# Layer 1 in a written order, with its last sums bank by bank; layer 3's rows one bank behind; shorter layernorm runs

## The chip, the cores and the metric

One core of one Trainium2 chip runs the whole program. The core has TensorE (PE, matrix products into PSUM), VectorE (DVE, elementwise), ScalarE (ACT, activation functions and copies), GpSimd (POOL), and the SP queue, which issues most DMAs. An engine works through its own queue in order, and semaphores tie the queues together. The metric is the time of one execution on the device in microseconds; the kernel before takes 1995.79 us (median of 3 runs, 1994.71 to 1996.02).

## The reference, cut to what matters

Four graph layers on N = 2708 nodes with D = 128 features share one matrix `adj` (2708 x 2708, about 2.3% filled). After each comes a layernorm. The change is in layers 1 and 3.

```python
def _L1_gnn_ref(node_features, adj_matrix, recency_prior, ...):   # recency_prior is adj again
    messages = node_features @ W_msg + b_msg
    logits = (messages @ W_q) @ (messages @ W_k).T / scale + gate_bias
    gates_masked = sigmoid(logits) * adj_matrix * recency_prior
    aggregated = gates_masked @ messages
    updated = relu(concatenate([node_features, aggregated], axis=1) @ W_upd + b_upd)
    ...                                             # layernorm, gamma, beta
# layer 3: n = adj @ x; s = n @ W + b; x1 = s * sigmoid(s); the same again on x1;
# then x + the second result, layernorm, and this is the output
```

The kernel adds a residual, `x + layernorm(...)`, and normalises it again. Layer 0 sums a gelu over pairs of neighbours. Layer 2 works on all pairs in hyperbolic geometry, with a small "bias point" made of `L2_gnn_b` and two attention vectors. All arithmetic of layers 1 to 3 that matters here is float32.

## The kernel before, in words

Rows are cut into NT = 22 tiles of 128 (the last has 20), and the 2708 columns into six banks: five of 512 and one of 148, each a PSUM bank. A float32 product of 128x512 shows up in the profile as two PE records.

**Two ways of ordering.** Inside `tc.manual_schedule()` each engine gets its instructions as the Python text issues them. Elsewhere a planner orders them by its own priorities, so that later work may be placed among earlier work. Layer 0's loop, layer 2's pairs and ends, and layer 3 have a written order. Layer 1 is left to the planner.

**Layernorm.** `normalize` (lines 199 to 218) turns the even and odd statistics of `bn_stats` into a scale r and an offset per row: a chain of 13 short DVE instructions with one square root on ACT in the middle (`Values.sqrt` takes one Newton step after it). Then each tile of the run is scaled and shifted by one instruction: every third tile on ACT (line 216), the others on DVE (line 218). `Resnorm.all` does two runs of 11 tiles: `add` (normalise h, times gamma, plus xb, statistics of the sum) for both, then `end` (normalise x) for both. Layer 0's end calls the same parts by hand.

**Layer 1, start (lines 979 to 1003).** Per group of four tiles: transposes of x, a copy by ACT (xT), the product with W_msg (mT, bias added by ACT), the product with the joined W_q W_k (qT, copied by DVE) and the rows of messages `mrow` (line 1002, one product of 128 columns per tile).

**Layer 1, loop (lines 1011 to 1030).** For every tile j: load the rows of adjT; six products `lg` (line 1024), each turned into a sigmoid by ACT (line 1025); two DVE multiplications by `at` over all 2708 columns (lines 1027 and 1028); six products into one PSUM tile `acc` of six banks (line 1030). `lg` has two PSUM buffers, `w` has two SBUF buffers, `at` three. `Weights2` (lines 290 to 327) prepares layer 2's bias point: DMAs on SP and POOL, some twenty small DVE instructions, two ACT functions and two products; the text calls it at tiles 5, 11 and 16, and the planner places it.

**Layer 1, end (lines 1031 to 1046).** DVE copies the six banks to aggT; 44 products (xT with the upper and aggT with the lower half of W_upd, line 266) give the rows of h; DVE adds the bias, ACT takes relu, DVE the statistics; then `Resnorm.all`.

**Layer 3 (lines 1473 to 1594).** Twice: nT = x^T adjT summed over 22 tiles in six PSUM banks (line 1543). Ten tiles of adjT are held in SBUF, the others are streamed. The last tiles (3 in the first pass, 6 in the second) are taken bank by bank. `Swish.step(k)` follows bank k: ACT copies bank k (line 1502), PE multiplies bank k-1 by W (line 266), DVE adds the bias (line 268) and ACT takes the sigmoid (line 1512); the rows of bank k-2 are finished: in the first pass one multiplication, in the second pass (`finish`, lines 1564 to 1576) multiplication, residual, statistics and, whenever at least 8 tiles are complete, `normalize` and the output DMA.

At the very end the count of cases that layer 0's fast way could not handle is read by every engine (line 1600), and a branch skips the slow way.

Of the kernel before, what the change touches and what calls it, by code (L numbers as in the profile page):

```python
# [20 lines left out]
P = 128  # L21
# [18 lines left out]
def gnn_stack(ctx: ExitStack, tc: tile.TileContext, t, out: bass.AP):  # L40
# [158 lines left out]
    def normalize(dst, src, st, a, b, V, sq=None):  # L199

        even, odd = st[:, a:b, 1], st[:, a:b, 4]
        d = V.tt(even, odd, ALU.subtract)
        q = V.new(d)
        nc.vector.scalar_tensor_tensor(q, d, 0.25, d, op0=ALU.mult, op1=ALU.mult)  # L204
        m = V.tt(st[:, a:b, 2], st[:, a:b, 5], ALU.add)
        nc.vector.scalar_tensor_tensor(q, m, 1.0 / D, q, op0=ALU.mult, op1=ALU.add)  # L206
        r = V.recip(V.sqrt(V.ts(q, LN_EPS, ALU.add)))
        mu = V.ts(V.tt(even, odd, ALU.add), 0.5, ALU.mult)
        if sq is not None:
            nc.vector.scalar_tensor_tensor(sq[:, a:b], q, float(D), V.mul(r, r), op0=ALU.mult, op1=ALU.mult)  # L210
        off = V.new(d)
        nc.vector.scalar_tensor_tensor(off, mu, -1.0, r, op0=ALU.mult, op1=ALU.mult)  # L212
        for i in range(a, b):
            c = slice(i - a, i - a + 1)
            if i % 3 == 2:
                nc.scalar.activation(dst[:, i, :], src[:, i, :], AF.Identity, bias=off[:, c], scale=r[:, c])
            else:
                nc.vector.tensor_scalar(dst[:, i, :], src[:, i, :], r[:, c], off[:, c], op0=ALU.mult, op1=ALU.add)  # L218
# [71 lines left out]
    class Weights2:  # L290
        def __init__(self, pool):
            self.pool = pool

        def load(self):
            nc.sync.dma_start(out=w2[:, :D], in_=t["L2_WT"])
            self.vecs = self.pool.tile([P, 3, D], F32, name="y2_vecs")
            self.cols = self.pool.tile([P, 3], F32, name="y2_cols")
            for k, name in enumerate(("L2_gnn_b", "L2_gnn_att_wl", "L2_gnn_att_wr")):
                nc.gpsimd.dma_start(out=self.vecs[:, k, :], in_=t[name].partition_broadcast(P))
                nc.sync.dma_start(out=self.cols[:, k:k + 1], in_=t[name].rearrange("(p o) -> p o", o=1))  # L300
            self.w_rows = self.pool.tile([P, D], F32, name="y2_w_rows")
            self.prods = self.pool.tile([P, 3, D], F32, name="y2_prods")

        def products_with(self, dst, v):
            nc.vector.tensor_tensor(self.prods, self.vecs, v[:, None, :].to_broadcast([P, 3, D]), op=ALU.mult)
            nc.vector.tensor_reduce(dst, self.prods, AX.X, ALU.add)

        def turn(self, ps):
            nc.tensor.transpose(ps[:, :D], w2[:, :D], ident)
            nc.vector.tensor_copy(self.w_rows, ps[:, :D])  # L310

        def bias_point(self):
            V = Values(self.pool, "y2_")
            vecs, cols = self.vecs, self.cols
            sums3 = self.pool.tile([P, 3], F32, name="y2_sums")
            self.products_with(sums3, vecs[:, 0, :])
            bn = V.norm(sums3[:, 0:1])
            bth = V.act(bn, AF.Tanh)
            bk = V.mul(V.mul(bth, V.recip(bn)), V.shrink(bth))
            nc.vector.tensor_scalar(y, vecs[:, 0, :], bk, None, op0=ALU.mult)  # L320
            nc.vector.tensor_copy(vecs[:, 0, :], y)
            nc.vector.tensor_tensor(cols[:, 0:1], cols[:, 0:1], bk, op=ALU.mult)
            self.products_with(yw, y)

        def columns(self, ps):
            nc.tensor.matmul(ps[:, :3], self.w_rows, self.cols, start=True, stop=True)
            nc.vector.tensor_copy(w2[:, D:], ps[:, :3])
# [631 lines left out]
    def layers_1_to_3(top):  # L959

        with ExitStack() as l1:
# [6 lines left out]
            mrow = wp.tile([P, NT, D], F32, name="mrow")  # L968
# [7 lines left out]
            with ExitStack() as pre:  # L976
                psum = pre.enter_context(tc.tile_pool(name="ps_pre1", bufs=2, space=PSUM))

# [10 lines left out]
                for a, b, r in groups():  # L989
# [12 lines left out]
                    sums(mrow[:r, a:b, :], a, b, r, [(xT, w_msg)], psum, msg_br)  # L1002
                nc.gpsimd.tensor_tensor(xb, x, over_tiles(beta), op=ALU.add)

            with ExitStack() as att:
                gp = att.enter_context(tc.tile_pool(name="gates", bufs=2))
                pacc = att.enter_context(tc.tile_pool(name="ps_agg1", bufs=1, space=PSUM))
                plog = att.enter_context(tc.tile_pool(name="ps_log", bufs=2, space=PSUM))
                acc = pacc.tile([P, N], F32, name="acc")
                weights2 = Weights2(wp)  # L1010
                for j, r in enumerate(rows):
                    at = stream.tile([P, N], F32, name="at")
                    nc.sync.dma_start(out=at[:r, :], in_=adjT[j * P:j * P + r, :])
                    if j == NT // 4:
                        weights2.load()
                    elif j == NT // 2:
                        weights2.turn(plog.tile([P, BANK], F32, name="lg"))
                        weights2.bias_point()
                    elif j == NT * 3 // 4:
                        weights2.columns(plog.tile([P, BANK], F32, name="lg"))  # L1020
# [452 lines left out]
        with ExitStack() as l3:  # L1473
# [20 lines left out]
            class Swish:  # L1494
# [24 lines left out]
                def step(self, k):  # L1519

                    if k < len(banks):
                        self.out_of(k)
# [111 lines left out]
```

## Time and profile before

| what | us |
|---|---|
| median of 3 runs | 1995.79 |
| the profiled execution's own time | 1993.64 |
| its span, first to last instruction | 1991.8 |
| layer 0 with its layernorm, until x is complete | 0 to 930.4 |
| layer 1's start, until the last of the first tile's `lg` | 931.9 to 970.0 |
| layer 1's loop, first `lg` to last `acc` | 948.7 to 1196.4 |
| layer 1's end, from there to the first transpose for layer 2 | 1196.4 to 1235.3 |
| layer 2, until layer 3's first product | 1235.3 to 1747.9 |
| layer 3, until the issue of the last output DMA | 1747.9 to 1984.0 |

PE is busy for 84% of the span, DVE for 77%, ACT for 55%. The page's slices show each engine's busy share over time; the timeline shows single instructions with their start, duration and, in brackets, the idle time of the engine before them and what ended it.

### The profile page before, as it was taken

The page shows a single profiled execution, that of the slowest core. Times are in us where ns is not written, and L with a number is a line of the kernel's source. Part 1 is how long each engine was busy: PE and PEld are TensorE (multiplying, and loading weights), DVE is VectorE, ACT ScalarE, POOL GpSimd, SP SyncE. Part 2 cuts the span into 40 slices and gives each one's busy share as a digit, 9 for nine tenths or more (in the row PEclk, how much of TensorE's full clock was granted, in tenths as well). Part 3 has the DMA queues.
Part 4 walks back from the last instruction along what each step waited for, and adds up shares of the span by engine and source line. Part 5 has one row for each costly group of instructions (what it writes and reads, how often), then busy time and mean ns, then how long its engine had stood idle before and what let it go on. Part 6 is the DMA issues. An engine that isn't in the chain of part 4 may idle for free. (4 is left out here: it accounts for less than half of the span.)

```text
span 1991.8 us, 36394 instructions
## 1 busy us (share of the span) xinstructions
PE 1663.9 (84%) x14037; PEld 949.8 (48%) x14037; DVE 1526.7 (77%) x3500; ACT 1103.2 (55%) x1519; POOL 679.0 (34%) x429
## 2 busy tenths in 40 slices
PE   5899999999999999871999994689898983089995
PEld 4666666666666666550444334322232321044542
DVE  7899999999999999876564658699999997810105
ACT  3666676666666666542433323599998983300103
POOL 5677677677577677461000000021000350000000
PEclk9899999999999999995999996779998986589998
DMA  8666666666666676432243310022222217034330
GB/s 224 150 130 135 138 139 128 136 141 127 136 148 122 136 147 111 82 66 88 114 141 139 127 45 1 1 87 88 75 81 95 81 42 293 0 144 167 112 116 30
DMA packets 218359, 222.25 MB, mean 112 GB/s; under 512 B 28373, under 2 KB 204475, under 8 KB 211715
## 3 DMA queue, kind: packets, MB, share of 16 engines
q1 hardware_dynamic: 167038, 195.95, 32.4%
q0 software_dynamic: 51136, 23.88, 10.3%
q8 instruction: 112, 1.84, 0.4%
q14 instruction: 73, 0.59, 0.1%
HBM read 211.94 MB, written 7.83 MB: 110 GB/s over the span
## 5 line engine op out<-in xcount | busy, mean ns | idle before, releaser
L722 POOL DMA_INDIRECT far<-d_tab,ix x352 | 561.8, 1596 | 259.2 <-DVE W L823 112.8
L836 ACT ACTIVATE g<-sl 128x768 f32<-128x768 f32 x484 | 393.4, 813 | 257.9 <-PE sl L763 238.1
L758 PE MATMUL sl<-dA,S 124*128 124x153 f16 x4840 | 408.8, 232 | 10.3 <-DVE W L823 7.8
L758 PEld LDWEIGHTS <-S 124*128 124x128 f16 x4840 | 331.1, 98 | 80.2 <-issue 68.4
L774 PE MATMUL acc<-g,W 128*32 128x128 f32 x4840 | 206.0, 278 | 0.5 <-DVE W L823 0.5
L1227 POOL TENSOR_TENSOR at<-at,off 128x128 f32<-128x128 f32 (+1 forms) x22 | 70.3, 3213 | 336.0 <-DVE m L1256 171.4
L1543 PE MATMUL acc<-held,x 128*128 128x512 f32 (+1 forms) x240 | 99.5, 563 | 84.1 <-DVE x L218 84.1
L774 PEld LDWEIGHTS acc<-g,W 128*32 128x32 f32 x4840 | 140.9, 109 | 58.6 <-issue 54.6
L763 PE MATMUL sl<-s,same 50*128 50x384 f16 x968 | 162.0, 308 | 0.0
L268 DVE TENSOR_TENSOR g<-ps,row_L_gnn_b 128x512 f32<-128x512 f32 (+2 forms) x14 | 7.9, 573 | 197.0 <-PE ps L266 196.9
L1025 ACT ACTIVATE w<-lg,row_L_gnn_gate_bias 128x512 f32<-128x512 f32 (+1 forms) x132 | 80.8, 635 | 137.7 <-PE lg L1024 74.3
L1283 PE MATMUL accV<-m,X 128*128 128x512 f32 (+4 forms) x264 | 128.4, 628 | 33.6 <-DVE m L1273 29.2
L823 DVE TENSOR_TENSOR W<-sl,own 128x150 f32<-128x150 f32 x484 | 143.3, 300 | 14.3 <-ACT g L836 13.6
L1235 PE MATMUL ps<-XT 128*128 128x512 f32 (+4 forms) x264 | 143.2, 626 | 3.1 <-ACT m L1240 2.8
L648 DVE TENSOR_SCALAR S<-rk 124x1000 f16<-124x1000 bf16 (+1 forms) x330 | 134.0, 431 | 0.0
L718 DVE FIND_INDEX8 ix<-v,o 128x8 uint32<-128x2728 f32 x44 | 131.7, 2994 | 0.0
L1024 PE MATMUL lg<-qT,mT 128*128 128x512 f32 (+2 forms) x264 | 115.6, 567 | 18.6 <-ACT w L1025 9.9
L1027 DVE TENSOR_TENSOR w<-w,at 128x2708 f32<-128x2708 f32 (+1 forms) x22 | 65.5, 2975 | 79.3 <-ACT w L1025 79.3
L736 DVE SCALAR_TENSOR_TENSOR extra<-far,v,extra 128x128 f32<-128x128 f32 x330 | 115.0, 349 | 6.3
L1543 PE MATMUL acc<-at,x 128*128 128x512 f32 (+3 forms) x288 | 116.8, 552 | 0.0
L680 DVE SCALAR_TENSOR_TENSOR o<-ps,ar 128x496 f32<-128x496 f32 x132 | 82.4, 624 | 37.3 <-PE ps L669 30.0
L1502 ACT COPY nT<-acc 128x512 f32<-128x512 f32 (+1 forms) x12 | 6.4, 531 | 186.5 <-PE acc L1543 186.5
(319 smaller groups left out, 2675.7 us busy)
## 6 DMA issues: line engine op xcount, KB each, us to landing
at<-in_adjT SPq DMA_DIRECT2D x40, 1354.0 KB
ar<-in_adj SPq DMA_DIRECT2D x105, 248.0 KB
far<-s_tab SPq DMA_DIRECT2D x44, 512.0 KB
at<-in_adjT SPq DMA_DIRECT2D x42, 448.0 KB
at<-in_adjT SPq DMA_DIRECT2D x21, 704.0 KB
at<-in_adjT SPq DMA_DIRECT2D x21, 650.0 KB
held<-in_adjT SPq DMA_DIRECT2D x10, 1354.0 KB
at<-in_adjT SPq DMA_DIRECT2D x21, 280.0 KB
```

Source lines behind the costliest of these rows:

```text
L648: nc.vector.tensor_scalar(self.S[h][:, :n, :, k * RG:(k + 1) * RG], self.rk[h][:, :n, :LR].rearrange("p b (c i) -> p b c i", c=NC), EDGE + ...
L718: nc.vector.max_index(ix, self.v[:, n * 8:n * 8 + 8], self.o.rearrange("p b j -> p (b j)"))
L722: nc.gpsimd.indirect_dma_start(out=self.far[n][:, k, :], out_offset=None, in_=d_tab[:, :], in_offset=bass.IndirectOffsetOnAxis(ap=self.ix[ ...
L758: nc.tensor.matmul(group[c], self.S[h][:, n, c, :], dA[q][:, b, c, :], start=c % 3 == 0 and q == 0, stop=False)
L763: nc.tensor.matmul(out, same[p], self.s3[p, :e - a, :], start=False, stop=True)
L774: nc.tensor.matmul(self.acc[q:q + 32, k, :], W[:, c, :], g[:, c, :], start=b == 0 and k == 0, stop=ends)
L823: nc.vector.tensor_tensor(W[:, :, :RG].rearrange("p (k c) i -> p k c i", k=2), columns_of(sl, D, DA), own[:, None, None, :].to_broadcast([ ...
L836: nc.scalar.activation(g.rearrange("p (k c) d -> p k c d", k=2), columns_of(sl, 0, D), AF.Gelu, scale=1.0 / D_SCALE)
L1024: nc.tensor.matmul(lg[:r, :b - a], mT[:, j * P:j * P + r], qT[:, a:b], start=True, stop=True)
L1235: nc.tensor.matmul(ps, XT[:, self.js], XT[:, c], start=True, stop=False)
L1283: nc.tensor.matmul(accV[:, a:b], X[:self.r, self.j, :], self.m[:, a:b], start=first, stop=last)
L1543: nc.tensor.matmul(acc[k], src[:rows[j], j, :], at[:rows[j], a:b], start=j == order[0], stop=j == order[-1])
```

## The change

- `normalize` computes half the root directly, so that the chain has 10 DVE instructions (11 and two more where the squared norm is wanted) in place of 13. Odd tiles go to ACT, even ones to DVE: five or six of 11 to ACT, where it was three or four.
- Layer 1's start multiplies each tile of xT by W_msg and the upper half of W_upd side by side (256 columns) and adds both biases at once: `both` holds the messages and the part of h that comes from x.
- Layer 1's loop, end and layernorm get a written order. `lg` of tile j and `acc` of an earlier tile alternate bank by bank. The tile summed lags by one, then two, then three tiles. The two multiplications follow each sigmoid, per bank (12 DVE instructions per tile instead of 2). The last three tiles' sums come at the end, bank by bank, followed by ACT's copy, the update products of the bank before and its relu and statistics. `w` has four buffers.
- `Weights2` becomes a generator that is taken one step further after each tile from tile 2 on; its three vectors are loaded by SP instead of POOL.
- Layer 3: the products, sigmoid and rows of bank k-1 all come after the first third of bank k's last products, and the copy of bank k after all of these.
- The read of the bad count is written before layer 3. In the engines' own queues it still stands where it stood, after the last output DMA on SP and after the last layernorm instruction on DVE and ACT.

```diff
 def normalize(dst, src, st, a, b, V, sq=None):
-        q = V.new(d)
-        nc.vector.scalar_tensor_tensor(q, d, 0.25, d, op0=ALU.mult, op1=ALU.mult)
-        m = V.tt(st[:, a:b, 2], st[:, a:b, 5], ALU.add)
-        nc.vector.scalar_tensor_tensor(q, m, 1.0 / D, q, op0=ALU.mult, op1=ALU.add)
-        r = V.recip(V.sqrt(V.ts(q, LN_EPS, ALU.add)))
-        mu = V.ts(V.tt(even, odd, ALU.add), 0.5, ALU.mult)
...
+        q = stt(d, 1.0 / 16.0, d, ALU.mult, ALU.mult)
+        if sq is None:
+            m = stt(m2, LN_EPS * D, m5, ALU.add, ALU.add)
+            w = stt(m, 0.25 / D, q, ALU.mult, ALU.add)
...
+        root = V.act(w, AF.Sqrt)
+        both = V.tt(even, odd, ALU.add)
+        r = V.recip(V.add(root, V.mul(w, V.recip(root))))
+        off = stt(both, -0.5, r, ALU.mult, ALU.mult)
...
-            if i % 3 == 2:
+            if i % 2:
                 nc.scalar.activation(dst[:, i, :], src[:, i, :], AF.Identity, bias=off[:, c], scale=r[:, c])
 # layer 1
-                    sums(mrow[:r, a:b, :], a, b, r, [(xT, w_msg)], psum, msg_br)
+                    for i in range(a, b, 2):
+                        m = min(i + 2, b)
+                        ps = psum.tile([P, 2, 2 * D], F32, name="ps_w")
+                        for k in range(i, m):
+                            nc.tensor.matmul(ps[:r, k - i, :], xT[:, k * P:k * P + r], w_both, start=True, stop=True)
+                        nc.vector.tensor_tensor(both[:r, i:m, :], ps[:r, :m - i, :], over_tiles(b_both, m - i, r),
+                                                op=ALU.add)
...
+                def gates(j, k):
...
+                    nc.tensor.matmul(lg, mT[:, j * P:j * P + r], qT[:, a:b], start=True, stop=True)
+                    nc.scalar.activation(w, lg, AF.Sigmoid, bias=gate_b[:r, :], scale=1.0 / math.sqrt(D))
+                    nc.vector.tensor_mul(w, w, at)
+                    nc.vector.tensor_mul(w, w, at)
+                def add_up(j, k):
+                    a, b = banks[k]
+                    nc.tensor.matmul(acc[k], mrow[:rows[j], j, :], ws[j][:rows[j], a:b], start=j == 0, stop=j == NT - 1)
+                def update(k):
+                    for a, b, r in of_bank(k):
+                        ps = plog.tile([P, BANK], F32, name="lg")[:r].rearrange("p (i d) -> p i d", d=D)
+                        for i in range(a, b):
+                            nc.tensor.matmul(ps[:, i - a, :], aggT[:, i * P:i * P + r], upd_a, start=True, stop=True)
+                        g = h[:r, a:b, :]
+                        nc.vector.tensor_tensor(g, g, ps[:, :b - a, :], op=ALU.add)
+                        nc.scalar.activation(g, g, AF.Relu)
...
+                with tc.manual_schedule():
+                    load(0)
+                    load(1)
+                    summed = 0
+                    for j in range(NT):
+                        if j + 2 < NT:
+                            load(j + 2)
+                        lag = 1 if j < NT // 3 else 2 if j < NT * 2 // 3 else LAST     # LAST = 3
+                        for k in range(len(banks)):
+                            gates(j, k)
+                            if j - summed >= lag:
+                                add_up(summed, k)
+                        summed += j - summed >= lag
+                        if j > 1:
+                            next(made, None)                                           # weights2
+                    for k, (a, b) in enumerate(banks):
+                        for j in range(summed, NT):
+                            add_up(j, k)
+                        nc.scalar.copy(aggT[:, a:b], acc[k])
+                        if k > 0:
+                            update(k - 1)
+                        if k > 1:
+                            look(k - 2)                                                # statistics
+                    update(len(banks) - 1)
+                    look(len(banks) - 2)
+                    look(len(banks) - 1)
+                    norm.all()
 # layer 3
                 def rows(self, k):
+                    self.products(k)
                     for a, b, r, g, gate in self.jobs.pop(k):
                         self.then(a, b, r, g, gate)
...
                 for k in range(len(banks)):
-                    for j, at in ats:
+                    for n, (j, at) in enumerate(ats):
                         product(k, j, at)
-                    swish.step(k)
+                        if k > 0 and n == len(ats) // 3:
+                            swish.rows(k - 1)
+                    swish.out_of(k)
...
+            before_end()                     # counts.append(nc.values_load(bad_n[0:1, 0:1]))
```

## The prediction

> **What bounds the kernel now.** I read the page's slices first, then the timeline of layer 1, then layer 3's two ends. Chances below are for faster or slower by more than 0.2% (4 us), about what a measurement of this kernel can tell from no change.
>
> Layer 1, timeline:
>
> ```profile
> 947.44 0.56 DVE L305 TENSOR_TENSOR y_prods<-y_vecs 128x384 f32<-128x384 f32 x1 [7.80 <-DMA y_vecs<-in_L_gnn_att_wr]
> 948.65 2.08 PE L1024 MATMUL lg<-qT,mT 128*128 128x512 f32 x2 [8.45 <-DVE qT L1001]
> ...
> 1032.54 5.19 PE L1024 MATMUL lg<-qT,mT 128*128 128x512 f32 x12 [0.53 <-ACT w L1025]
> 1040.07 9.49 PE L1030 MATMUL acc<-w,mrow 128*128 128x512 f32 x24
> 1044.87 1.27 ACT L1025 ACTIVATE w<-lg,row_L_gnn_gate_bias 128x512 f32<-128x512 f32 x2 [6.39 <-PE acc L1030]
> 1053.10 5.19 PE L1024 MATMUL lg<-qT,mT 128*128 128x512 f32 x12 [0.53 <-ACT w L1025]
> ...
> 1196.41 3.30 DVE L1032 COPY aggT<-acc 128x512 f32<-128x512 f32 x6 [7.44 <-PE acc L1030]
> 1199.86 0.77 PE L266 MATMUL ps<-w_L_gnn_W_upd,xT 128*128 128x128 f32 x2 [3.49 <-DVE h L1040]
> 1214.35 0.15 DVE L204 SCALAR_TENSOR_TENSOR v<-v 128x11 f32<-128x11 f32 x1
> 1234.78 2.14 DVE L218 TENSOR_SCALAR x<-x,v,v 128x128 f32<-128x128 f32 x8
> 1235.26 2.58 PE L247 MATMUL ps<-ident,x 128*128 128x128 f32 x11 [22.90 <-DVE x L218]
> 1246.03 0.16 DVE L140 TENSOR_SCALAR w<-xsq 128x22 f32<-128x22 f32 x1
> ```
>
> At the start PE stands 8.45 us: the copy of qT is queued on DVE behind y_prods, which waits for POOL's vector loads. In the loop two tiles take 20.56 us (1032.54 to 1053.10), 10.28 each; PE bounds it, with small waits. From the last `acc` (1196.3) to layer 2's chain (1246.03) the work is serial: copies, 44 products, statistics, layernorm.
>
> The same kind of product without waits is in layer 3:
>
> ```profile
> 1747.85 4.33 PE L1543 MATMUL acc<-held,x 128*128 128x512 f32 x6 [84.09 <-DVE x L218]
> 1765.48 7.73 PE L1543 MATMUL acc<-held,x 128*128 128x512 f32 x12
> 1873.67 4.71 PE L1543 MATMUL acc<-held,x 128*128 128x512 f32 x12
> ```
>
> Twelve records, one tile's six banks, take 4.6 us at full clock (1864.48 to 1873.67 holds two tiles: 4.6 each). The row at 1765.48 is the clock: PE had run at full speed since 1751 and without a pause falls to half speed for 10 us.
>
> Layer 3's end, and the layernorm's prices:
>
> ```profile
> 1951.95 0.68 DVE L1565 TENSOR_TENSOR g<-g,gate 128x512 f32<-128x512 f32 x1
> 1952.66 0.69 DVE L1566 TENSOR_TENSOR x<-x,g 128x512 f32<-128x512 f32 x1
> 1963.40 0.88 ACT L216 ACTIVATE x<-x,v,v 128x128 f32<-128x128 f32 x2 [1.56 <-DVE v L212]
> 1963.40 1.63 DVE L218 TENSOR_SCALAR x<-x,v,v 128x128 f32<-128x128 f32 x6
> 1983.07 0.97 SPq L1576 DMA_DIRECT2D out<-x  x1
> ```
>
> A normalised tile costs 0.27 us on DVE, 0.42 on ACT. A 128x512 DVE instruction is followed by a dependent one after 0.71 us.
>
> **The change part by part**, against the profiled execution (1993.64 us: span 1991.8 and 1.84 around it; the median is 2.15 above).
>
> *Layer 0's layernorm, −3.1.* Four runs. The chain took 2.72 us (920.97 to 923.69); three dependent steps of 0.2 go: −0.65 each, −2.6. Of 11 tiles, DVE did 8 or 7 (2.14, 1.88 us) beside ACT's 3 or 4; now ACT does 5 or 6 (2.06, 2.47) and is the slower. In the two `add` runs the gamma product waits for it (−0.1, +0.6); in the two `end` runs DVE goes on early (−0.5 each). PE, which starts behind the bad count on DVE, starts layer 1 at 928.8 instead of 931.9.
>
> *Layer 1's start.* PE's work: 22 transposes of 0.12, two 2708-column products of 4.6 and 22 products of 256 columns at 0.43: 21.2 us. Around it 1.7 for the small weights before and 2.5 for filling and draining the chain. ACT (1.3 per group) and DVE (2.1) lie under PE's 3.9. POOL's five short instructions come before xb (6.12 us) and end before first use, some 6 us later. The y stall is gone: SP loads these vectors inside the loop, behind load(4). Cold clock: bounds 1.7 (half of one 3.4 us phase, as at 1747.85) and 6.8 (the second, 10 us phase too); I take 4.5. `lg` starts at 928.8 + 29.9 = 958.7.
>
> [...]
>
> *The loop.* 44 half tiles of 4.6: 202.4 (by the waitless row; this loop's own 9.33 for two would give 205.3, the computed column rate 199.5). The three tiles without sums (0, 7, 14) leave PE at ACT's pace, 0.5 each; updates of banks 0 to 3 add 3.6. Last `acc` at 1166.2 (before 1196.3). Covers: ACT 4.1 us per tile; DVE 10 pieces of 512 at 0.60 to 0.73 and two short ones, 7.1 to 8 of 9.2; the steps of weights2 add at most 2 on DVE and two table loads of 1.28 on ACT, each in a tile of its own. Loads: 1354 KB per 9.2 us is 150 GB/s, the slices show 407 GB/s in such a load; slack is about a tile. If cover failed, PE would wait at each `acc`.
>
> [...]
>
> *Layer 1's end.* After the last `acc` only the short bank remains: copy 0.5, products 0.5, add 0.5, relu 0.5, statistics 0.8. The layernorm starts at 1169.0 instead of 1214.35: −45.3.
>
> *Its layernorm, +4.8.* Before, the planner mixed both runs and DVE had no hole: 20.4 us (1214.35 to 1234.78). Written out, they queue: chain 2.06, rows 2.1, gamma 1.65, sum 1.65, statistics 2.2; again with six ACT rows 2.5: 10.1; third chain with the squared norm and a 0.91 memset 3.55: 23.3 in all, +2.9. In the last run ACT's six rows delay its copies for layer 2's weights: +1.9. Bounds 0 and +7. Layer 2's chain starts 40.5 earlier; its pairs are DVE-bound and keep their length.
>
> *Layer 2's end, −1.4.* Two runs as above; layer 3's first product needs tile 0 of the second: −0.65 twice, −0.5 from DVE, +0.44 because its root queues behind ACT's rows.
>
> *Layer 3's end, +1.7.* ACT's order now has the rows of tiles 0–7 before the copy of bank 2, and those of 8–15 before bank 4's. Stepping through with the durations above (in the old base): bank 2 is summed at 1951.1, its copy is done at 1956.7, PE stands 3.0; bank 4's copy ends at 1972.45, PE stands 4.9. Then bias 1973.75, table 1.28, sigmoid 0.63, three rows of 0.7 to 0.9, the two short groups 2.3, chain 2.06, ACT's three tiles 1.26: last DMA at 1984.8 instead of 1983.07. Bounds −1 (no blocking, one chain shorter) and +8 (both stalls in full).
>
> *Bad count, 0:* the queues keep it at the end.
>
> Sum: −40.5 − 1.4 + 1.7 = −40.2 (the −3.1 is inside). Profiled 1953.4, median 1955.6.
>
> **Rivals.**
> A, the old pace (12%): interleaving makes each product wait on two engines, or DVE's pieces cost over 0.8 us. At 10.28 per tile: 22 × 1.08 = 24 back, 1979. For it: waits of 0.5 per tile now; against: layer 3's unbroken rows, DVE's slack.
> B, in-order ACT (6%): both blockings cost their bounds: +6.3 and +2.2: 1964.
> C, slower (3%): PE at full load loses its clock in the loop as at 1765.48. Each 10 us half-speed phase costs 5.1 us; from eight such phases in 200 us on the gain is gone, ten give 2007. Against: layer 3 runs 200 us at full clock behind its second phase.
>
> **How the numbers follow.** Main case 79%: 1955.6, its own range 1945 to 1967. Bounds added up: loop −2.9/+2.9, clock −2.8/+2.3, layernorm −4.8/+2.2, layer 3 −2.7/+6.3: 1942.4 to 1969.3. With part of A (half the old pace, 1967.6) and B: 1943 to 1971. Faster 0.96, same 0.01, slower 0.03.
>
> **What would show it.** No PE idle of 8 us near 940; `lg` from about 959; 9.2 us per tile; last `acc` 1166; layer 2's chain near 1205; PE waits of 3 and 5 us for nT at layer 3's end, last DMA under 2 us later relative to layer 3's start. Wrong: a tile period over 9.6, DVE idle on `at`, half-clock phases inside the loop.

## The result, and the profile after

| | before | after |
|---|---|---|
| median, us (range of 4 runs each) | 1995.88 (1994.71 to 1996.02) | 1962.22 (1960.28 to 1962.80) |
| profiled execution, us (its span) | 1993.64 (1991.8) | 1961.88 (1960.2) |

The ratio is 0.9833 (95% interval 0.9821 to 0.9845): 33.7 us faster by the medians, 31.6 by the two spans. The forecast was 1955.6 within 1943 to 1971, so the sign and the range held, and 6.6 us of the forecast gain did not come (8.5 us between the profiled executions, 1961.88 for 1953.4). Divided at the same places in both traces, the profiled executions differ so:

| stretch | before | after | difference | forecast |
|---|---|---|---|---|
| until layer 0's layernorm begins | 896.29 | 897.81 | +1.5 | 0 |
| layer 0's layernorm, to the product of the bad count | 35.18 | 31.86 | −3.3 | −3.1 |
| layer 1 to the first step of its layernorm | 282.88 | 247.32 | −35.6 | −42.2 |
| its layernorm and layer 2, to layer 3's first product | 533.50 | 537.05 | +3.6 | +3.4 |
| layer 3, to the issue of its last output DMA | 235.22 | 238.51 | +3.3 | +1.7 |
| from there to the end of the span | 8.73 | 7.65 | −1.1 | 0 |

The first row is code that the change doesn't touch; over all runs of this study it lies between 895.7 and 899.4. In the kernel before, three first steps of layer 1's layernorm already stand among the statistics, from 1212.79 on; the stretch there ends at 1214.35, as in the prediction, where the chain goes on. The two misses are in layer 1 and in layer 3.

Layer 1 of the kernel after, timeline (start, duration, engine, line, operation; in brackets the idle time before and what ended it):

```profile
958.61 1.98 PE L1063 MATMUL lg<-qT,mT 128*128 128x512 f32 x4 [0.27 <-DVE qT L1026]
959.81 1.28 ACT L1064 ACT_TABLE_LOAD   x1 [2.02 <-PE lg L1063]
...
965.66 1.12 PE L1063 MATMUL lg<-qT,mT 128*128 128x512 f32 x2 [0.53 <-ACT w L1064]
...
974.85 1.02 PE L1063 MATMUL lg<-qT,mT 128*128 128x512 f32 x2
...
983.93 1.02 PE L1063 MATMUL lg<-qT,mT 128*128 128x512 f32 x2
...
1015.59 1.13 PE L1063 MATMUL lg<-qT,mT 128*128 128x512 f32 x2 [0.31 <-ACT w L1064]
...
1021.35 5.09 PE L1063 MATMUL lg<-qT,mT 128*128 128x512 f32 x12
1026.96 1.13 PE L1063 MATMUL lg<-qT,mT 128*128 128x512 f32 x2 [0.53 <-ACT w L1064]
...
1142.60 1.04 PE L1063 MATMUL lg<-qT,mT 128*20 128x512 f32 x2
...
1153.06 6.25 PE L1070 MATMUL acc<-w,both 128*128 128x148 f32 x14
...
1160.24 2.93 PE L1070 MATMUL acc<-w,both 128*128 128x512 f32 x6
...
1164.10 2.93 PE L1070 MATMUL acc<-w,both 128*128 128x512 f32 x6
...
1176.99 0.15 DVE L129 TENSOR_TENSOR v<-st 128x11 f32<-128x11 f32 x1
```

The stand of 8.45 us for qT is gone. A whole tile takes 9.09 us (974.85 to 983.93), where it was 10.28. Three things cost more than forecast. ACT's table load sits between the first product and its sigmoid, so tile 0 takes 7.05 us (958.61 to 965.66). The last tile, with 20 rows, takes 10.46 from its first gate to the last sum between its gates (1142.60 to 1153.06). The cycle of a bank at the end is 3.86 (1160.24 to 1164.10).

Two stretches of the same loop as windows (bounds, length, then each engine's busy time and count in the order PE, weight loads, DVE, ACT, POOL; granted clock as a share of full speed, DMA share, GB/s):

```profile
974.90:1058.80 83.90, 82.84 (x217) 38.21 (x217) 72.67 (x135) 38.69 (x61) 0.00 (x0) 1.00 0.45 156
1058.80:1142.60 83.80, 83.27 (x221) 38.83 (x219) 70.75 (x115) 36.50 (x58) 0.00 (x0) 1.00 0.36 131
```

PE is busy for 99% of them at the full clock, 1.00, and DVE for 84 to 87%.

Layer 3's start, timeline, and then windows over its middle two rows:

```profile
1714.04 11.40 PE L1604 MATMUL acc<-held,x 128*128 128x512 f32 x24 [82.65 <-ACT x L228]
1725.38 6.36 PE L1604 MATMUL acc<-at,x 20*128 20x512 f32 x12
1731.67 6.60 PE L1604 MATMUL acc<-held,x 128*128 128x512 f32 x12
```

```profile
1725.40:1728.50 3.10, 3.10 (x9) 1.39 (x9) 0.00 (x0) 0.00 (x0) 0.00 (x0) 1.00 0.00 0
1728.50:1731.70 3.20, 3.20 (x7) 1.35 (x5) 0.00 (x0) 0.00 (x0) 0.00 (x0) 0.50 0.00 0
1731.70:1735.00 3.30, 3.30 (x5) 1.48 (x5) 0.00 (x0) 0.00 (x0) 0.00 (x0) 0.50 0.72 233
```

The half-speed phase that the prediction showed at 1765.48 is here too, from 1728.50 on, with PE busy all the time. It begins within the row of the tile that has only 20 rows (20*128).

Layer 3's end, timeline, and windows behind PE's two stands:

```profile
1920.13 1.65 ACT L228 ACTIVATE x<-x,v,v 128x128 f32<-128x128 f32 x4 [1.11 <-DVE v L205]
1921.68 0.56 ACT L1571 COPY nT<-acc 128x512 f32<-128x512 f32 x1
1922.30 1.44 PE L278 MATMUL ps<-w_L_gnn_W,nT 128*128 128x128 f32 x8 [2.48 <-ACT nT L1571]
1923.53 4.38 PE L1604 MATMUL acc<-at,x 128*128 128x512 f32 x6
...
1939.61 2.08 PE L278 MATMUL ps<-w_L_gnn_W,nT 128*128 128x128 f32 x8 [4.31 <-ACT nT L1571]
```

```profile
1922.30:1925.00 2.70, 2.70 (x10) 1.91 (x11) 0.69 (x1) 0.46 (x1) 0.00 (x0) 0.64 0.60 194
1925.00:1927.90 2.90, 2.90 (x6) 0.68 (x4) 1.36 (x2) 1.46 (x2) 0.00 (x0) 0.75 0.00 0
...
1939.60:1943.00 3.40, 3.39 (x13) 3.10 (x14) 0.69 (x1) 0.51 (x1) 0.00 (x0) 0.50 0.48 154
```

ACT's four rows stand ahead of the copy of nT, and PE waits 2.48 and later 4.31 us, about as forecast (3.0 and 4.9). Not forecast is what follows: the clock is 0.64 and 0.50 behind these stands, so that eight products of 128 columns take 1.44 and 2.08 us instead of the 1.05 of the banks before them.

### The profile page after: what moved, and what is told of

It is laid out like the page before. It is cut to its first block, busy times and chain, and to the rows that moved or that the text cites. A ratio compares the mean times of both kernels' runs of the same rounds, so it can differ in the third digit from the quotient of the medians.

```text
span 1960.2 us, 36493 instructions
## 1 busy us (share of the span) xinstructions
PE 1662.2 (85%) x13993; PEld 952.3 (49%) x13993; DVE 1549.8 (79%) x3657; ACT 1119.8 (57%) x1551; POOL 676.7 (35%) x431
## 4 chain that ended last, share of the span: by engine, by line
DVE 41%; PE 31%; POOL 9%; issue 7%; DMA 6%; ACT 6%; SPq 0%; DVEq 0%; ACTq 0%; POOLq 0%
PE acc L1604 10%; POOL far L739 8%; PE lg L1063 5%; PE acc L1070 5%; DVE ix L735 5%; DMA far<-d_tab,ix 3%; DVE W L840 3%; DVE u L1322 3%; DVE w L1336 3%; DVE m L1325 3%; DVE extra L753 2%; DVE o L697 2%; DVE m L1339 2%; DVE m L1342 2%; PE sl L775 2%
## 5 line engine op out<-in xcount | busy, mean ns | idle before, releaser
L1063 PE MATMUL lg<-qT,mT 128*128 128x512 f32 (+2 forms) x264 | 121.2, 547 | 3.6 <-ACT w L1064 3.1
L1070 PE MATMUL acc<-w,both 128*128 128x512 f32 (+2 forms) x264 | 121.2, 547 | 0.0
L1604 PEld LDWEIGHTS acc<-held,x 128*128 128x128 f32 x240 | 45.0, 196 | 134.8 <-ACT x L228 82.9
```

The lines of the kernel that those rows point to most:

```text
L1063: nc.tensor.matmul(lg, mT[:, j * P:j * P + r], qT[:, a:b], start=True, stop=True)
L1070: nc.tensor.matmul(acc[k], mrow[:rows[j], j, :], ws[j][:rows[j], a:b], start=j == 0, stop=j == NT - 1)
L1604: nc.tensor.matmul(acc[k], src[:rows[j], j, :], at[:rows[j], a:b], start=j == order[0], stop=j == order[-1])
```

## The experiments

Kernels are the one after with the edit shown, unless another is named. Pieces of time come from the profiled executions. In brackets stand the ratio to the kernel before and its 95% interval. Layer 2, of which only the edit of `normalize` touches a part, takes 499.4 to 502.3 us from its chain to layer 3's first product without a cause that I can name, so totals that differ by 2 us are not read; stretches are.

**The 20-row tile of layer 1 as 128 rows** (the added columns are zero).

```diff
-            mT = wp.tile([P, N], F32, name="mT")
+            mT = wp.tile([P, NT * P], F32, name="mT")
+                nc.gpsimd.memset(mT[:, N:], 0.0)
...
-                    nc.tensor.matmul(lg, mT[:, j * P:j * P + r], qT[:, a:b], start=True, stop=True)
+                    nc.tensor.matmul(lg, mT[:, j * P:(j + 1) * P], qT[:, a:b], start=True, stop=True)
...
-                    nc.tensor.matmul(acc[k], mrow[:rows[j], j, :], ws[j][:rows[j], a:b], start=j == 0, stop=j == NT - 1)
+                    nc.tensor.matmul(acc[k], mrow[:, j, :], ws[j][:, a:b], start=j == 0, stop=j == NT - 1)
```

> The changed kernel, with layer 1's last row tile (20 rows) carried as 128: mT has 108 more columns of zeros, its products and its sigmoid take 128 partitions, and the sums take all 128 rows of w against message rows that are zero behind row 20. The two multiplications stay at 20 rows. Theory A: PE loses about 0.2 us at each change between weights of 20 and of 128 rows, because the next weights are then not loaded beside the running product; so tile 21 takes 9.1 us instead of 10.5 and a bank at the loop's end 3.45 instead of 3.86. Layer 1's layernorm starts at about 1173.3 instead of 1177.0, and the span is 3.7 us shorter, 1956.5. Theory B: these stretches wait for the gates of the last tile (ACT, then DVE); then the periods stay 10.5 and 3.86 and the span stays at 1960.

Measured: 1956.33 us (0.9815, 0.9799 to 0.9831). Its timeline at layer 1's end:

```profile
1143.62 1.02 PE L1064 MATMUL lg<-qT,mT 128*128 128x512 f32 x2
...
1152.46 5.56 PE L1071 MATMUL acc<-w,both 128*128 128x148 f32 x14
...
1158.75 2.74 PE L1071 MATMUL acc<-w,both 128*128 128x512 f32 x6
...
1162.22 2.74 PE L1071 MATMUL acc<-w,both 128*128 128x512 f32 x6
```

The last tile takes 8.84 us between the same two places (1143.62 to 1152.46), as any full tile, where it took 10.46; a bank's cycle is 3.47 instead of 3.86. From the first `lg` to the layernorm it is 214.19 us instead of 218.38. So 4.2 of the missing microseconds are the 20 rows, as theory A had it: the work is less, but each change between weights of 20 and of 128 costs PE time, about 0.2 us by the two changes in a bank's cycle. What happens at a change is seen best in the next run.

**Layer 3: the eight tiles' normalisation after the next copy.** `finish` returns the normalisation and its output DMA as a function, and the loop calls it behind `out_of`.

```diff
+                    later = []
                     for n, (j, at) in enumerate(ats):
                         product(k, j, at)
                         if k > 0 and n == len(ats) // 3:
-                            swish.rows(k - 1)
+                            later = swish.rows(k - 1)
                     swish.out_of(k)
+                    for f in later:
+                        f()
```

> The changed kernel, with one order altered in layer 3: the layernorm of eight tiles and its output DMA are issued after the copy of the bank that is being summed, not before it. Theory A: PE's two idle times at the end (2.5 and 4.3 us) and the half clock behind them come from copies of nT that queue on ACT behind the layernorm's root and rows. Without them a bank takes 6.4 us throughout, the products of bank 4 start near 1930 instead of 1939.6, and the last output DMA is 6 to 9 us earlier: span 1952 to 1954. Theory B: the end is bound by the chain on DVE and ACT (bias, gate, rows, statistics, layernorm), and the idle times of PE lie beside it: PE's idle times go and the span loses 2 us or less.

Measured: 1951.88 (0.9793, 0.9776 to 0.9809); layer 3 takes 231.22 instead of 238.51. Bank after bank takes 6.43 us (copies at 1901.75, 1908.19, 1914.62), without a stand; one of 4.40 us is left, at the last short bank. So ACT's rows ahead of the copy, with the lower clock behind them (0.50 to 0.75 in the kernel after), cost 7.3 us (theory A). Against the kernel before, layer 3 is 4.0 us shorter. The weight loads of this run, within one bank:

```profile
1899.21 0.19 PEld L1604 LDWEIGHTS acc<-at,x 128*128 128x128 f32 x1 [0.24 <-issue]
1899.64 0.19 PEld L1604 LDWEIGHTS acc<-at,x 128*128 128x128 f32 x1 [0.24 <-issue]
1900.59 0.29 PEld L1604 LDWEIGHTS acc<-at,x 20*128 20x128 f32 x2 [0.76 <-issue]
1901.64 0.30 PEld L1604 LDWEIGHTS acc<-held,x 128*128 128x128 f32 x2 [0.76 <-issue]
```

Loads of 128 rows start 0.43 us apart. The load of 20 rows starts 0.95 after the one before it, and the next one of 128 rows has the same 0.76 of idle time ahead of it.

**Layer 3 in its old order, with the new `normalize`.**

```diff
                 def rows(self, k):
-                    self.products(k)
...
+                def step(self, k):
+                    if k < len(banks):
+                        self.out_of(k)
+                    if 0 < k <= len(banks):
+                        self.products(k - 1)
+                    if k > 1:
+                        self.rows(k - 2)
...
-                        if k > 0 and n == len(ats) // 3:
-                            swish.rows(k - 1)
-                    swish.out_of(k)
+                    swish.step(k)
```

> The changed kernel with layer 3's steps in the order of the kernel before (copy, products of the bank before, rows of the one before that, all at the end of a bank). Theory A: the new order itself makes layer 3 longer, by 3.3 us from first product to last output DMA, and 4 us when the shorter layernorm run is counted; so the span falls to about 1956. Theory B: the 3.3 us come from where layer 3 falls in the clock's cold phases, then the span stays at 1960 within 1 us.

Measured: 1954.36 (0.9798, 0.9782 to 0.9814); layer 3 takes 231.82, 6.7 less than after. From bank 0's copy to the last DMA issue it is 42.50 us, against 44.79 before (old order, old `normalize`) and 48.34 after. So in the old order the shorter `normalize` brings 2.3 there, and with it the new order costs 5.8; the result showed only their sum, +3.55. The two can't simply be added: with the old function in the new order (a run below) the same stretch is 47.44, shorter than after.

**Layer 1 planned instead of in the written order.** The pieces per bank, the lag and the four buffers stay.

```diff
-                with tc.manual_schedule():
+                with ExitStack():
                     load(0)
```

> The changed kernel with the same loop of layer 1, bank by bank and with the same lags, but given to the planner instead of kept in the written order. Theory A: the gain in the loop comes from its structure (multiplications in pieces per bank, a whole tile between gates and sums, four w buffers) and PE binds it at 9.1 us per tile under either order; the layernorm's two runs are mixed again, which saves 2.5 us: span 1957 to 1961. Theory B: the written order is what keeps PE fed, and the planner's order gives back the old period of 10.28 us: 22 x 1.2 = 26 us longer, 1986.

Measured: 1952.20 (0.9793, 0.9777 to 0.9809), span 1947.9, better than either theory had it. From the first `lg` to layer 3's first product it is 744.73 us, 10.7 less than after. Its timeline (PE where the lag grows; DVE near the end):

```profile
1018.09 5.08 PE L1063 MATMUL lg<-qT,mT 128*128 128x512 f32 x12
1023.01 1.02 PE L1070 MATMUL acc<-w,both 128*128 128x512 f32 x2
...
1165.02 0.16 DVE L129 TENSOR_TENSOR v<-st 128x11 f32<-128x11 f32 x1
```

The planner puts a sum behind the six gates, where the written order has the next gate and its wait of 0.53; such things bring 3.3 us in the loop. The first steps of the layernorm (1165.02) begin while PE still works on the last banks; from the end of the statistics to layer 2's chain it is 29.7 us instead of 35.7, so 6.0 less, which the next run has too. The remaining 1.4 lies in layer 2. The old pace does not come back: between such places a tile takes 9.09 here too. So the gain of the loop is the pieces, the lag and the buffers together; the fixed order itself costs some 9 us.

**Only the layernorm planned.**

```diff
-                    norm.all()
+                norm.all()
```

> The changed kernel with layer 1's layernorm given to the planner, the loop still in its written order. Theory A: written out, the layernorm's two runs queue and DVE stands while ACT does its rows; mixed by the planner it loses these holes, so the time from the layernorm's first step to the chain of layer 2 that reads M's statistics falls from 35.7 us to about 32.5 and the span by 2.5 to 4.5 us: 1956 to 1958. Theory B: the planner now has ACT do every other row, so ACT is the later one in either order and the span stays within 1 us.

Measured: 1954.32 (0.9794, 0.9778 to 0.9811). From the end of the sums' statistics to layer 2's chain it is 29.6 us instead of 35.7, more than the 2.5 to 4.5 of theory A. Its timeline:

```profile
1177.25 0.38 ACT L145 ACTIVATE v<-v 128x11 f32<-128x11 f32 x2
...
1178.68 2.39 DVE L230 TENSOR_SCALAR both<-both,v,v 128x128 f32<-128x128 f32 x9
1178.73 4.34 ACT L228 ACTIVATE both<-both,v,v 128x128 f32<-128x128 f32 x11 [1.10 <-DVE v L205]
```

Both runs' roots follow each other, and their rows are one block: nine on DVE beside eleven on ACT. In the written order the second run's chain began at 1186.70, 9.7 us behind the first.

**The old `normalize` in the new kernel.** Lines 199 to 218 of before take the place of the new function.

```diff
-        q = stt(d, 1.0 / 16.0, d, ALU.mult, ALU.mult)
...
+        nc.vector.scalar_tensor_tensor(q, d, 0.25, d, op0=ALU.mult, op1=ALU.mult)
+        m = V.tt(st[:, a:b, 2], st[:, a:b, 5], ALU.add)
+        nc.vector.scalar_tensor_tensor(q, m, 1.0 / D, q, op0=ALU.mult, op1=ALU.add)
+        r = V.recip(V.sqrt(V.ts(q, LN_EPS, ALU.add)))
...
-            if i % 2:
+            if i % 3 == 2:
```

> The changed kernel with the function normalize of the kernel before (13 steps on DVE instead of 10, every third row on ACT instead of every other). Theory A: each run's chain costs 0.65 us more where it is on the path: two of four in layer 0 (1.8 us in all), two to four in layer 1 (1.3 to 2.6), 1.5 in layer 2, 0.65 in layer 3: span 5 us longer, 1965. Theory B: fewer rows on ACT give back what the longer chain costs, because ACT's rows delay the gamma product (by 0.5 to 1.1 us in each of layer 1's runs) and, in layer 3, the copies of nT behind them: 1960 to 1962.

Measured: 1967.80 (0.9865, 0.9848 to 0.9881). Layer 0's layernorm is 3.32 longer, layer 1's 2.06, layer 3 0.3. The span is 6.0 longer, 1.36 of it before layer 0's layernorm. That is near theory A. In layer 3 theory B has a part: PE's first stand there is a little shorter, and the clock stays full behind it (timeline, window):

```profile
1929.18 1.16 PE L266 MATMUL ps<-w_L_gnn_W,nT 128*128 128x128 f32 x8 [2.36 <-ACT nT L1559]
```

```profile
1929.20:1932.60 3.40, 3.40 (x14) 1.84 (x14) 0.91 (x2) 1.44 (x2) 0.00 (x0) 1.00 0.48 154
```

From this stand to the next bank's products it is 6.54 us (1929.18 to 1935.72), where the kernel after takes 8.23 (1922.30 to 1930.53).

**Sigmoid's table early.** One sigmoid ahead of the loop, to load the table while PE still makes qT.

```diff
+                early = rp.tile([P, 1], F32, name="early")
                 with tc.manual_schedule():
+                    nc.scalar.activation(early, gate_b, AF.Sigmoid)
```

> The changed kernel with one more sigmoid, of one column, on ACT ahead of layer 1's loop. Theory A: the first tile's gates stand because ACT loads its table (1.28 us) only when the first product is there, at 959.81; loaded before, the first sigmoid starts near 959.8 instead of 961.10 and everything behind it is 1.2 us earlier: span 1959. Theory B: the first tile is bound by the two product buffers and the 0.9 us round trip between PE and ACT, and 0.3 us or less are gained.

Measured: 1961.30 (0.983, 0.9814 to 0.9847), and from the first `lg` to the layernorm 218.36 instead of 218.38. Its timeline of ACT says why:

```profile
893.76 0.20 ACT L1091 ACTIVATE early<-row_L_gnn_gate_bias 128x1 f32<-128x1 f32 x1
...
960.16 1.28 ACT L1064 ACT_TABLE_LOAD   x1 [2.02 <-PE lg L1063]
```

The sigmoid was placed 66 us ahead, among layer 0's last work, where the next function loads its own table at once (1.28 us at 893.98). The run tests neither theory; the version that does is below.

**The kernel before, its three vectors on SP.**

```diff
-                nc.gpsimd.dma_start(out=self.vecs[:, k, :], in_=t[name].partition_broadcast(P))
+                nc.sync.dma_start(out=self.vecs[:, k, :], in_=t[name].partition_broadcast(P))
```

> The kernel before, with one edit: the three vectors for layer 2's bias point are loaded from SyncE's queue instead of GpSimd's. Theory A: the 8.45 us stall of PE at 948.65 is the wait for these vectors, and it is on the path: the loop starts 7 to 8.5 us earlier and the span is 7 to 8.5 us shorter, 1984. Theory B: the time comes back in the loop, which is fed by ACT and DVE and not only by PE, or the vectors are late on the other queue too: 1989 to 1992.

Measured: 1984.41 (0.9952, 0.9936 to 0.9969), and from the product of the bad count to layer 3's first product 9.6 us less than in the kernel before, 7.9 of it ahead of the first `lg`. The stand of 8.45 us is gone, and the first `lg` rows take 1.02 to 1.13 instead of 2.08. Alone, this line of the change brings 10 us of what the whole brings, 34.

**The 20-row tile early in layer 3's second pass** (on top of the deferred normalisation).

```diff
-                order = back[:STREAM] + in_turns("hfhfhfhffhfhhhhhfff", near_by, back[STREAM:])
+                order = back[:STREAM] + in_turns("hfhfhfhffhfhhhhhfff", near_by, back[-1:] + back[STREAM:-1])
```

> The changed kernel with the copy of nT ahead of the layernorm (as in the run before with that order), and one more edit: in layer 3's second pass the row tile of 20 rows is taken fourth instead of last, so it is no longer one of the six tiles that are summed bank by bank. Theory A: the loss of 0.2 us at each change between weights of 20 and 128 rows holds here too: each of the five long banks takes 6.02 us instead of 6.43, and the last output DMA, counted from layer 3's first product, is 1.6 to 2.1 us earlier than in that run (231.2 us). Theory B: the 0.41 us belong to the reading of the bank's last sum (copy, then products), not to the 20 rows: the bank stays at 6.43 and the 231.2 us stay.

Measured: 1955.07 (0.9802, 0.9785 to 0.9818), where it was 1951.88 without the edit. The banks at the end do fall to 6.04 us, as theory A had it, but layer 3 takes 233.01 instead of 231.22. Timeline, and windows of 2 us from the second half of the 20-row tile on:

```profile
1843.42 5.72 PE L1604 MATMUL acc<-at,x 20*128 20x512 f32 x12
1849.08 7.24 PE L1604 MATMUL acc<-held,x 128*128 128x512 f32 x12
```

```profile
1845.40:1847.40 2.00, 2.00 (x5) 0.77 (x5) 0.00 (x0) 0.00 (x0) 0.00 (x0) 0.94 0.00 0
1847.40:1849.40 2.00, 2.00 (x5) 0.99 (x4) 0.00 (x0) 0.00 (x0) 0.00 (x0) 0.50 0.00 0
1849.40:1851.40 2.00, 2.00 (x3) 0.85 (x3) 0.00 (x0) 0.00 (x0) 0.00 (x0) 0.50 0.68 200
```

In the second pass here PE loses its clock (0.50 from 1847.40 on) after 100 us at full clock (1.00 from 1735 to 1843). In the first pass of every kernel but the last one below, where this tile is also taken as a whole, it takes 6.03 to 6.98 us with its 20 rows, and full tiles without a lower clock take 4.71; the windows of the kernels before and after show 0.50 there. Its products come without a pause (PE is busy for 2.00 of every 2.00 us above); what sets them apart is that they use 20 of 128 rows.

**Three together:** layer 1 planned with the layernorm, its last tile padded, layer 3's copy first.

> Three edits to the changed kernel at once: layer 1's loop and layernorm given to the planner, its last tile carried as 128 rows, layer 3's copy of nT ahead of the layernorm. Theory A: they act in different stages and add up. Counted from the first gate product to layer 3's first product 755.4 - 10.7 - 3.7 = 741 us, and layer 3 231.2 us instead of 238.5: span about 1938 (1936 to 1941). Theory B: the planned order already hides part of what the 20 rows cost, so 2 to 3 us less are gained: 1941 to 1943.

Measured: 1939.74 (0.9724, 0.9708 to 0.974). First `lg` to layer 3's first product 741.46, layer 3 231.25: the parts add up.

**These three, the short tile early, and the table.** Beside the order shown above, a sigmoid that reads the last column of mT, so that it can't be placed earlier than that.

```diff
+                early = rp.tile([P, 1], F32, name="early")
+                nc.scalar.activation(early, mT[:, N - 1:N], AF.Sigmoid)
                 with ExitStack():
```

> The kernel with these three edits, with two more: layer 3's tile of 20 rows taken early, and one sigmoid of one column that reads the last column of mT, so that it cannot be placed ahead of the copies of layer 1's start and ACT's table is there for the first gates. Theory A: 1.6 to 2.1 us less in layer 3 and 1.2 us less in the first tile (its first sigmoid starts when the first product is done, without the 1.28 us of the table): span 1934 to 1936. Theory B: the first tile is bound by the two product buffers, and the table's load only moves the waiting: 0.3 us there, span 1936 to 1937.

Measured: 1940.61 (0.9727, 0.9711 to 0.9743). The table does what was claimed of it: tile 0's gates are one row of 5.18 us from the first `lg` on, and the loop's gates end 1.33 us earlier (188.05 against 189.38 from the first `lg`). It doesn't show in the total: layer 3 takes 233.29, as in the run with the tile moved (233.01), and layer 2 was 1.8 longer.

**The three, and layer 3's short tile as 128 rows.**

```diff
                         at = last[j] = stream.tile([P, N], F32, name="at")
+                        if rows[j] < P:
+                            nc.gpsimd.memset(at, 0.0)
                         nc.sync.dma_start(out=at[:rows[j], :], in_=adjT[j * P:j * P + rows[j], :])
...
-                    nc.tensor.matmul(acc[k], src[:rows[j], j, :], at[:rows[j], a:b], start=j == order[0],
+                    nc.tensor.matmul(acc[k], src[:, j, :], at[:, a:b], start=j == order[0],
```

> The kernel with the three edits (planned loop and layernorm, layer 1's last tile as 128 rows, copy of nT ahead of the layernorm), with one more: in layer 3 the tile of 20 rows is also carried as 128, its adjacency buffer cleared on GpSimd before its load. It keeps its place as third tile of the first pass and last of the second. Theory A: PE's second half-clock phase, which starts 4 us into the 20-row tile (in the first pass, and in the run before this in the second pass too, where that tile had been moved), is caused by products on 20 rows; with 128 rows it is gone: the four tiles behind layer 3's first product take 20.7 us instead of 24.4, the banks at the end 6.02 instead of 6.43, layer 3 takes 225.5 to 226 us instead of 231.2 and the span is about 1934. Theory B: the second phase belongs to the start, 10 to 14 us behind the first product whatever is computed: the four tiles stay at 24.4, only the banks get shorter, layer 3 takes 229.5 and the span is 1937 to 1938.

Measured: 1932.62 (0.9692, 0.9674 to 0.9709), the fastest version of the study. The timeline of layer 3's start:

```profile
1700.41 11.75 PE L1607 MATMUL acc<-held,x 128*128 128x512 f32 x24 [82.56 <-ACT x L228]
1712.00 4.71 PE L1607 MATMUL acc<-at,x 128*128 128x512 f32 x12
1716.54 4.71 PE L1607 MATMUL acc<-held,x 128*128 128x512 f32 x12
1721.08 4.71 PE L1607 MATMUL acc<-at,x 128*128 128x512 f32 x12
```

The row at 1712.00 is the tile that took 6.36 us at 1725.38 in the kernel after, and it and the next take 4.71 each. From the first product to 1721.08 it is 20.67 us, where the run "Three together" took 24.36 for the same four tiles. The cold start is still there (0.50 in the first 3.4 us), the second phase is gone with the 20 rows (1.00 from 1707.20 to 1725.60), and layer 3 takes 225.84 us (theory A).

## Why the prediction was right, and where not

**Right.** Layer 0's layernorm got 3.3 us shorter (3.1 forecast), and the run with the old function gives these 3.3 back. PE's wait for the y vectors went as described, and the kernel before with that one line changed shows its worth. A tile takes 9.09 us (9.2 forecast), and DVE keeps up: its pieces take 0.69 and 0.31 us, 7.5 in all per tile. The written layernorm queues (+3.9 us to layer 2's chain, +4.8 forecast), and the run that plans it shows that the order is the cause. Layer 2's end came 1.47 shorter (1.4 forecast). PE stands twice at layer 3's end.

The first `lg` at 958.61 (958.7 forecast) is in part luck. PE started layer 1 at 930.10, 1.3 later than forecast, because layer 0 itself was longer, and layer 1's start took 28.5 us instead of 29.9: the clock was 0.50 from 930.10 to 936.60 and 1.00 after that, which costs 3.2 us where 4.5 were taken and the bounds were 1.7 and 6.8.

**The loop, +8.1 us over its steps** (218.38 us from the first `lg` to the layernorm, 210.3 forecast). The mechanism held, the terms were mis-sized:
- "44 half tiles of 4.6" took the 20-row tile like any other, and the end had only its banks' work. The short tile's own 1.6 (10.46 against 8.84) and its part of the bank cycles come to 4.2 (the padded run).
- "The three tiles without sums leave PE at ACT's pace, 0.5 each" is right for two of them (5.61 each, counted with the 5.1 that a run of gates takes), but tile 0 takes 7.05: the table load, 1.28, was taken to lie beside other work. At tile 0 there is none yet. The run with the sigmoid behind mT's last column gets 1.33 of it back.
- A half tile takes 4.54, not 4.6; over 18 tiles that gave back 2.1. No run shows the "computed column rate" behind the 199.5 in the forecast's sum; 44 half tiles of 4.54 make 199.8. Waits such as the one at 1015.59, behind the table loads for `Weights2`' root on ACT (1.28 us each, at 1012.04 and 1013.55), and `Weights2`' own two small products on PE took 2.2. I argued this pair from the timeline, and no run isolates it.
- From the last sum to the layernorm it is 4.1 us (1172.9 to 1176.99), where 2.8 were forecast: ACT's and DVE's last serial steps. The planned loop doesn't shorten them; from the last gate to the end of the statistics both kernels take 24.2 us (1152.8 to 1177.1 in the kernel after). About 1 us of the 8.1 stays open.

**Layer 3's end, +1.8 us** (+3.55 from bank 0's copy to the last issue, +1.73 forecast). The step that put the products behind each stand at full clock was wrong: 0.64 and 0.75 were granted behind the first, 0.50 behind the second. Counted from bank 0's copy, bank 2's copy ends 0.4 us earlier than forecast, but bank 4's 1.2 later and the bias behind it starts 2.0 later; from there to the last DMA it is 10.83 where 11.05 were forecast (the durations listed for this add up to 10.5). The bound of −1 for an end without blocking was too cautious as well: with the copy first the end is 40.79, 4.0 us shorter than before.

**The row at 1765.48** I read as PE losing its clock "at full speed and without a pause" and rested rival C on it. That reading was wrong. The tile just before it has 20 rows, and the clock falls within that tile (kernel before, timeline and window):

```profile
1758.62 6.93 PE L1543 MATMUL acc<-at,x 20*128 20x512 f32 x12
```

```profile
1761.40:1764.80 3.40, 3.40 (x5) 1.33 (x4) 0.00 (x0) 0.00 (x0) 0.00 (x0) 0.50 0.00 0
```

The phase moves with that tile (0.50 from 1847.40 on in the early tile's run) and goes with its rows (1.00 from 1712.00 to 1725.60 in the run with 128 rows).

**The rivals.** A, the old pace, is refuted by the period of 9.09, also where the planner orders the loop. B gave 1964, closer to 1962.22 than the main case. Its blocking is there at nearly its price: the runs that take it away save 6.1 us (the planned layernorm) and 7.3 us (the copy first), where B's bounds were 7 and 8. But against the kernel before, the two stretches came out far below these bounds, because beside the blocking they gained 2.2 and 4.0 us, which B did not have; and B took the loop from the main case, 8.1 us too short. That these errors nearly cancel in its total is luck. C is refuted by the clock of 1.00 in all windows of the loop.

**Open:** the tail behind the last output DMA's issue is 6.2 to 7.8 us in all kernels made from the one after, and 8.65 to 8.73 in the two made from the one before. It isn't `normalize` nor layer 3's order, since the runs with the old ones have the short tail. The bad count is read after the last DMA in both. No run takes the pieces, the lag and the buffers of the loop apart, and none isolates the joined product of layer 1's start.

## What to carry to other kernels

Look at the short last tile before anything else: with 20 of 128 rows it was slower here than a full one, in layer 1 by changes of the weights' shape (10.46 us against 8.84) and in layer 3 by the clock (0.50), and filling it with zeros brought 4 us and 5 us. A PSUM copy that PE waits for belongs ahead of long ACT work in ACT's queue (7.3 us here), and the price of a stand of PE can include products at a lower clock behind it (0.64 and 0.75 behind the first one here, about 1.8 us). Splitting work into pieces and fixing their order are two changes: here the first, with the lag and the buffers, brought the loop's gain, and the second gave 9 us of it away, which one run with the order left to the planner tells.

## What the runs showed of the hardware that was not expected

- Within twelve records in a row of products on 20 rows the granted clock fell to 0.50, though PE had no idle time: at 1761.40 in the kernel before, at 1728.50 in the one after, at 1847.40 in the run with the tile moved; in the run where the tile has 128 rows the clock is 1.00 there (1712.00 to 1725.60).
- At a change between weights of 128 and of 20 rows the weight load started 0.95 us after the one before, where 0.43 lay between loads of 128 rows (the run with the copy first, 1899.21 to 1900.59). A change cost about 0.2 us, an estimate from the banks' cycles with two changes each: 3.86 against 3.47 in layer 1, 6.43 against 6.04 in layer 3.
- A stand of 2.48 us was followed by a lower clock (0.64 and 0.75 in the 5.6 us behind it). One of 2.36 us, with the old `normalize`, was not (1.00). ACT's copies of nT show the difference in time: in the kernel after, bank 2's starts 11.03 us behind bank 1's and bank 3's another 6.27 us later; in four other runs (the padded tile, the planned loop, the planned layernorm, the early table) these are 11.03 to 11.31 and 6.26 to 6.27; with the old `normalize` they are 10.92 and 4.58.
- Not the chip's doing, but as unexpected: an instruction with no late input, written ahead of a loop, was placed 66 us before that loop's first table load (893.76 against 960.16).
